# First layer of a four-layer graph kernel: which engine makes the constants, which steps of the plan are urgent, and what the normed tiles wait for

## Chip, cores and metric

The kernel runs on one core of a Trainium2 chip. The metric is the time of one execution on the device, in microseconds (us); lower is better. A profile comes from one further execution, whose span runs from the first to the last instruction that the profiler recorded. The core has five engines with queues of their own: TensorE (PE, with its weight loads as PEld), VectorE (DVE), ScalarE (ACT), GpSimd (POOL) and SyncE (SP, which issues the DMAs).

## What is computed

The input x is 128 graphs of 64 nodes with 256 features, in float32, and an adjacency matrix of 64 by 64. Four layers follow each other, each of the form x + f(relu(layernorm(x))). The change lies in the first one:

```python
h = jnp.maximum(_layernorm(x, axis=-1), 0.0)
A_norm = A + jnp.eye(n)
deg = jnp.sum(A_norm, axis=0) + jnp.sum(A_norm, axis=1) - jnp.diagonal(A_norm)
dinv = jax.lax.rsqrt(deg)
A_hat = A_norm * dinv[:, None] * dinv[None, :]
agg = jnp.einsum('nm,bmd->bnd', A_hat, h)
h1 = relu(batchnorm(agg @ W1.T + b1))        # 512 wide, over all rows
x = x + batchnorm(h1 @ W2.T + b2)
```

The second layer needs all eigenvectors of the normalized Laplacian of the same matrix (`eigh` of a 64 by 64 matrix). The third has four small LSTMs, the fourth an attention over edges; neither is touched by the change.

## The kernel before

**Tiling.** The 8192 rows of x are 16 blocks of 512 rows. A block is four tiles of 128 rows, each with two graphs, and stays in SBUF. A_hat is applied to a tile with a matrix of 128 by 128 that has A_hat twice on its diagonal (BDH). For one block, the first half of layer 1 (`hidden_block`) does this: four normed tiles on ScalarE (`relu`, written into z), eight matmuls with BDH for each half of the features (`mix`), a copy of the result into z on ScalarE, eight matmuls of 512 columns with W1 (`product`), statistics of these on VectorE (bn_stats into st1) and a copy on ScalarE. When all blocks are done, the statistics are put together, and `features0` does the products with W2.

**Layernorm's scales.** `norms` makes the scales (r, m) for a group of blocks: four bn_stats for each block, and then a dependent chain of twelve small steps, one of them a square root on ScalarE. Groups are block 0, blocks 1 to 3, and three of four blocks. In the trace the tiles of this chain are called m_st, m_d, m_v, m_y, m_r and m_m.

**The eigenvectors** are a long serial chain of small steps beside this: `adjacency` makes the Laplacian S out of the degrees, `tridiagonal` turns it around with the matrix JR and does some 61 Householder steps (`householder`), then `vectors` finds values, vectors and a verdict (k_badi). At the end of the stage a branch reads the verdict and would run a slower method if it failed. The second layer starts after the branch.

**What sets the order.** The class `Plan` lays the instructions of TensorE, VectorE and ScalarE out by hand, before any is emitted, with estimated costs: `busy` is how long a step holds its engine, `ready` when its result can be used. `chain` places a step of the eigenvector chain at once. `beside` puts a step into its engine's queue. Before each step of the chain, `fill` places queued steps as long as they fit before the time at which the chain's step is due, with a tolerance (0.6 us on TensorE, 0.3 on the two others). An urgent step is preferred, and needs only to start before that time. `fill` looks at the first 12 entries of a queue. `event(t)` is a need that is met at planned time t. A step's needs count in the plan alone; the real waits come from the tiles that it reads and writes.

**The start.** `constants` makes index vectors with iota on GpSimd, and copies of parts of the identity matrix and some small index arithmetic on VectorE. It is emitted before the plan and isn't part of it. `adjacency` copies the identity matrix twice more (self.I2, called I in the trace). `rs`, `cs` and `dg` are row sums, column sums and the diagonal of the adjacency matrix. `dg`'s step writes the tile `junk` (f_a_junk). The steps of A_hat come last in `adjacency`: An is A + I, dd[:, 1] the diagonal matrix of dinv, `hat` a matmul of the two, Ah its scaled result, `both` a matmul that repeats it on both halves, and two copies write BDH.

The needs of the four normed tiles of a block are the scales, the products of three blocks before (for the buffer z), and `mixes`, which is the second of the BDH copies.

```python
if at is not None and (at + x.busy <= until + self.slack[engine] or x.urgent and at <= until):
    if best is None or (not x.urgent, at) < best[:2]:
        best = not x.urgent, at, x
```

```python
h = [beside("S", lambda j=j: relu(j), needs, 0.52, 0.6) for j in range(TPB)]
mixed = []
for dc in range(2):
    bank = []
    x = beside("T", lambda dc=dc: mix(dc), h, 0.98, 1.1, bank)
```

Of the kernel before, what the change touches and what calls it, by code (L numbers as in the profile page):

```python
# [11 lines left out]
ALU = mybir.AluOpType  # L12
# [900 lines left out]
class Fast:  # L913
# [36 lines left out]

    def constants(self):
        o, nc, k, t = self.o, self.nc, self.k, self.t
        iota = lambda x, pat, base, m: nc.gpsimd.iota(x, pattern=pat, base=base, channel_multiplier=m,
                                                      allow_small_or_imprecise_dtypes=True)
        ident = k.ident
        self.J = t("J", 128, 64)
        iota(self.J[:], [[1, 64]], 0, 0)
        self.P = t("P", 64, 1)  # L960
        iota(self.P[:], [[0, 1]], 0, 1)

        self.TR, self.TC = t("TR", 64, 64), t("TC", 64, 1)
        iota(self.TR[:], [[-1, 64]], 63, 0)
        iota(self.TC[:], [[0, 1]], 63, -1)
        self.JR = t("JR", 64, 64)
        o.copy(self.JR[:], ident[:64, 63::-1])
        self.I2 = t("I2", 64, 128)
        o.copy(self.I2[:, 0:64], ident[:64, :64])
        o.copy(self.I2[:, 64:128], ident[:64, :64])  # L970

        self.q, self.uw, self.ME = t("q", 128, 18, 4, 2), t("uw", 128, 4, 2), t("ME", 128, 2, 64)
        for x, v in ((self.q[:, 0, :, 0], 0.0), (self.q[:, 0, :, 1], 1.0), (self.q[:, 1, :, 0], 1.0),
                     (self.q[:, 1, :, 1], 0.0), (self.uw[:, 0, 0:1], 1.0), (self.uw[:, 0, 1:2], 0.0),
                     (self.ME[:, 1, 0:1], 0.0), (t("DR", 128, 2, 64)[:, 1, 63:64], 0.0)):
            nc.gpsimd.memset(x, v)
        self.I2T = t("I2T", 128, 64)
        o.copy(self.I2T[0:64, :], ident[0:64, 0:64])
        o.copy(self.I2T[64:128, :], ident[64:128, 64:128])
        self.one = t("one", 64, 64)  # L980
        nc.vector.memset(self.one[:], 1.0)
        self.low = t("low", 64, 64)
        o.ts(self.low[:], self.J[:64, :], self.P[:], ALU.is_lt)

        self.par = t("par", 64, 1)
        pi, pj = t("pi", 64, 1, dt=I32), t("pj", 64, 1, dt=I32)
        o.copy(pi[:], self.P[:])
        o.ts(pj[:], pi[:], 1, ALU.bitwise_and)
        o.copy(self.par[:], pj[:])
        o.ts(self.par[:], self.par[:], -2.0, ALU.mult, 1.0, ALU.add)  # L990

        self.dl = 4.0 / (GRID * GRID + 1)
        self.h = self.dl / (GRID - 2)
        X = self.X0 = t("X0", 128, 64)
        iota(X[0:64, :], [[1, 64]], 1, 64)
        iota(X[64:128, :], [[1, 64]], 1, 64)
        o.ts(X[:], X[:], self.dl, ALU.mult, -2.0, ALU.add)
        self.HN = t("HN", 128, 64)
        o.ts(self.HN[:], self.J[:], -0.5, ALU.add, self.h, ALU.mult)

# [463 lines left out]
class Kernel:  # L1466
# [60 lines left out]
    def adjacency(self, fast, plan):  # L1527


        nc, o = self.nc, self.o  # L1530
        t = lambda n, *s: fast.t("a_" + n, N, *s)
        I = self.ident[:N, :N]
        self.I2 = self.c("I2", N, P)
        o.copy(self.I2[:, 0:N], I)
        o.copy(self.I2[:, N:P], I)
        self.S = self.c("S", N, N)
        self.BDH = self.c("BDH", P, P)
        self.BDA, self.BDU, self.BDUT = (self.c(n, P, P) for n in ("BDA", "BDU", "BDUT"))
        nc.vector.memset(self.BDH[:], 0.0)
        for bd in (self.BDA, self.BDU, self.BDUT):  # L1540
            nc.gpsimd.memset(bd[:], 0.0)
        rs, cs, dg, deg, junk = t("rs", 1), t("cs", 1), t("dg", 1), t("deg", 2), t("junk", N)
        di, dm, pos, y, r = t("di", 2), t("dm", 2), t("pos", 1), t("y", 2), t("r", 2)
        dd, An, Ah, L = t("dd", 2, N), t("An", N), t("Ah", N), t("L", N)
        V = lambda emit, *needs, busy=0.09, ready=0.22: plan.chain("V", emit, needs, busy, ready)
        now = {}

        def keep(name, a, b, p=64):
            now[name] = fast.mm((a, b), p=p)

        came = plan.chain("T", lambda: None, (), 0.0, 3.0)
        d = V(lambda: o.red(rs[:], self.A[:], ALU.add), came)
        d = V(lambda: o.red(cs[:], self.AT[:], ALU.add), came)
        g = V(lambda: o.stt(junk[:], self.A[:], 1.0, I, ALU.mult, ALU.mult, acc=dg[:]), came, busy=0.2, ready=0.3)
        d = V(lambda: o.add(cs[:], cs[:], rs[:]), d)

        d = deg0 = V(lambda: o.sub(deg[:, 0:1], cs[:], dg[:]), d, g)
        d = V(lambda: o.ts(deg[:, 1:2], deg[:, 0:1], 1.0, ALU.add), d)
        m = d = V(lambda: o.ts(dm[:], deg[:], 1e-30, ALU.max), d)
        q = plan.chain("S", lambda: self.act(y[:], dm[:], AF.Sqrt), [d], 0.13, 0.25)  # L1560
        l = V(lambda: o.add(L[:], self.A[:], self.AT[:]), came)
        l = V(lambda: o.ts(L[:], L[:], -0.5, ALU.mult), l)
        l = V(lambda: o.stt(L[:], I, deg[:, 0:1], L[:], ALU.mult, ALU.add), l, deg0, ready=0.3)
        z = V(lambda: o.ts(pos[:], deg[:, 0:1], 0.0, ALU.is_gt), deg0)
        d = V(lambda: o.recip(r[:], y[:]), q)
        d = V(lambda: o.mul(r[:], r[:], dm[:]), d)
        d = V(lambda: o.add(r[:], r[:], y[:]), d)
        d = V(lambda: o.recip(r[:], r[:]), d)
        d = h = V(lambda: o.ts(di[:], r[:], 2.0, ALU.mult), d)
        d = z = V(lambda: o.mul(di[:, 0:1], di[:, 0:1], pos[:]), d, z)  # L1570
        d = V(lambda: o.ts(dd[:, 0, :], I, di[:, 0:1], ALU.mult), d, busy=0.15, ready=0.28)
        d = plan.chain("T", lambda: keep("s", L[:], dd[:, 0, :]), [d, l], 0.3, 0.5)
        made = V(lambda: o.ts(self.S[:], now["s"][:], di[:, 0:1], ALU.mult), d, busy=0.15, ready=0.28)

        V = lambda emit, *needs: plan.beside("V", emit, needs, 0.15, 0.3)
        a = V(lambda: o.add(An[:], self.A[:], I), came)
        d = V(lambda: o.ts(dd[:, 1, :], I, di[:, 1:2], ALU.mult), h)

        def hat():
            now["h"] = fast.psv.tile([P, N], F32, name="fvps")  # L1580
            self.mm(now["h"][:N, :], An[:], dd[:, 1, :])

        def both():
            now["b"] = fast.psv.tile([P, N], F32, name="fvps")
            self.mm(now["b"][:], self.I2[:], Ah[:])

        d = plan.beside("T", hat, [a, d], 0.3, 0.5)
        d = V(lambda: o.ts(Ah[:], now["h"][:N, :], di[:, 1:2], ALU.mult), d)
        d = plan.beside("T", both, [d], 0.3, 0.5)
        d = V(lambda: o.copy(self.BDH[0:64, 0:64], now["b"][0:64, :]), d)  # L1590
        return made, V(lambda: o.copy(self.BDH[64:128, 64:128], now["b"][64:128, :]), d)

    def eigenvectors(self):
# [2 lines left out]
        self.U, self.UT = self.c("U", N, N), self.c("UT", N, N)  # L1596
        with ExitStack() as ex:
            fast = Fast(self.tc, ex, self)
            fast.constants()
            plan = Plan(dict(T=0.6, S=0.3, V=0.3), 5)  # L1600
            made, mixes = self.adjacency(fast, plan)
            self.open0(ex)
            self.hidden0(plan, mixes)
# [187 lines left out]
    def hidden0(self, plan, mixes):  # L1791

        pool, used, banks = self.p0, {}, []
        for lo, hi in ((0, 1), (1, 4), (4, 8), (8, 12), (12, 16)):
            r, m, steps = self.norms(pool, range(lo, hi))
            came = [plan.event(4.5 + 1.5 * (i + (i > 0))) for i in range(lo, min(hi, 4))]
            d, first = [], (hi - lo) * TPB
            for n, (engine, emit) in enumerate(steps):
                if n < first:
                    d.append(plan.beside(engine, emit, [came[n // TPB]] if came else [], 0.36, 0.45, urgent=not lo))  # L1800
                else:
                    d = [plan.beside(engine, emit, d, 0.12, 0.25, urgent=not lo)]
            for i in range(lo, hi):
                banks += self.hidden_block(i, r[:, i - lo], m[:, i - lo], plan, d + used.get(i - 3, []) + [mixes], used)
        self.features0(plan, banks, used)

    def hidden_block(self, i, r, m, plan, needs, used):
        nc, pool, psum, W1 = self.nc, self.p0, self.ps0, self.W0[0]
        beside, now = plan.beside, {}

# [17 lines left out]
        mixed = []  # L1828
        for dc in range(2):
            bank = []  # L1830
            x = beside("T", lambda dc=dc: mix(dc), h, 0.98, 1.1, bank)
            x = beside("S", lambda dc=dc: self.act(now["z"][:, 2 + dc, :], now["m", dc][:], AF.Copy), [x], 0.55, 0.65)
            bank.append(x)
            mixed.append(x)
# [952 lines left out]
```

## Time and profile before

| | |
|---|---|
| Time before, median of 3 runs | 2326.83 us (2326.06 to 2328.2) |
| Profiled execution, its own time | 2326.85 us |
| Its span | 2325.1 us |
| First layer and eigenvectors, to the branch | 0 to 370.1 us |
| TensorE busy in 0 to 10 / 10 to 15 / 15 to 20 us | 1.03 / 1.88 / 4.42 us |
| TensorE busy in 100 to 300 us | 195.2 us |
| Loads of x, W1 and W2 | DMA engines full from 10 to 30 us, near 350 GB/s |
| Householder steps | from 11.5 to 272 us |
| Last product with W1 to first product with W2 | 208.3 to 217.6 us |

Line 799 is a helper that records every operation of the three ordered engines, so instructions are told apart by tiles: out<-in, with the names of the program. A row of a timeline has the start, the duration, the engine, the operation, shapes and how many instructions were merged, and in brackets the idle time of its engine before it with what ended it. A float32 matmul of the eigenvector chain shows up as two records, as does a product of 512 columns.

### The profile page before, as it was taken

The page shows a single profiled execution, that of the slowest core. Times are in us where ns is not written, and L with a number is a line of the kernel's source. Part 1 is how long each engine was busy: PE and PEld are TensorE (multiplying, and loading weights), DVE is VectorE, ACT ScalarE, POOL GpSimd, SP SyncE. Part 2 cuts the span into 40 slices and gives each one's busy share as a digit, 9 for nine tenths or more (in the row PEclk, how much of TensorE's full clock was granted, in tenths as well). Part 3 has the DMA queues.
Part 4 walks back from the last instruction along what each step waited for, and adds up shares of the span by engine and source line. Part 5 has one row for each costly group of instructions (what it writes and reads, how often), then busy time and mean ns, then how long its engine had stood idle before and what let it go on. Part 6 is the DMA issues. An engine that isn't in the chain of part 4 may idle for free.

```text
span 2325.1 us, 32725 instructions
## 1 busy us (share of the span) xinstructions
PE 2283.6 (98%) x12169; PEld 1633.1 (70%) x12169; DVE 1629.3 (70%) x4054; ACT 1139.5 (49%) x2483; POOL 3.0 (0%) x26
## 2 busy tenths in 40 slices
PE   7999998999999999999999999999999999999999
PEld 4554445676777788888999998888885544554544
DVE  8887676888447777666767676559756686766667
ACT  5765865754436654433444444336435544444321
POOL 0000000000000000000000000000000000000000
PEclk9999999999999999999999999999999999999999
DMA  5000211230000000001000002000010000000001
GB/s 171 1 1 26 65 56 30 71 83 19 1 37 0 1 19 1 1 1 37 1 1 1 1 1 73 1 1 17 1 46 28 1 5 15 15 19 14 14 24 46
DMA packets 61065, 54.81 MB, mean 24 GB/s; under 512 B 15203, under 2 KB 58724, under 8 KB 60900
## 3 DMA queue, kind: packets, MB, share of 16 engines
q1 hardware_dynamic: 60900, 52.66, 7.4%
q8 instruction: 97, 1.59, 0.3%
q14 instruction: 68, 0.56, 0.1%
HBM read 35.86 MB, written 16.78 MB: 23 GB/s over the span
## 4 chain that ended last, share of the span: by engine, by line
PE 79%; DVE 3%; issue 1%; ACT 1%; DMA 0%; SPq 0%; ACTq 0%; DVEq 0%
PE ps L799 69%; PE acc L799 5%; PE pt L799 4%; PE pe L799 1%; PE y L799 1%; DVE aw L799 1%; DVE X L799 1%; DVE sm_m L799 0%; DVE XV L799 0%; ACT ls_g L799 0%; ACT h L799 0%; DVE ls_g L799 0%; ACT big L799 0%; DVE ls_t L799 0%; DVE sm_e L799 0%
## 5 line engine op out<-in xcount | busy, mean ns | idle before, releaser
L799 ACT ACTIVATE ls_g<-ls_g,ls_b 128x512 f32<-128x512 f32 (+4 forms) x472 | 243.1, 565 | 151.4 <-DVE ls_g L799 149.6
L799 ACT ACTIVATE ls_g<-ps,ls_b 128x256 f32<-128x256 f32 (+3 forms) x268 | 115.5, 470 | 330.9 <-PE ps L799 327.7
L799 PE MATMUL ps<-z,w 128*128 128x512 f32 x512 | 254.9, 621 | 0.9 <-ACT z L799 0.9
L799 PE MATMUL ps<-big,X 128*128 128x176 f32 (+3 forms) x848 | 212.7, 366 | 0.1
L799 DVE TENSOR_TENSOR ls_g<-ls_z,ps 128x512 f32<-128x512 f32 (+5 forms) x256 | 146.8, 579 | 91.9 <-PE ps L799 90.4
L799 DVE TENSOR_TENSOR aw<-at,ed_OST 128x1024 f32<-128x1024 f32 x128 | 149.9, 1219 | 83.0 <-PE ps L799 82.8
L799 PE MATMUL ps<-ls_tx,X 128*128 128x160 f32 (+2 forms) x960 | 206.8, 326 | 0.6 <-ACT ls_g L799 0.6
L799 PE MATMUL ps<-X,X 128*128 128x160 f32 (+1 forms) x896 | 199.1, 306 | 0.0
L799 PE MATMUL ps<-X,ls_w 128*128 128x256 f32 x640 | 190.5, 379 | 0.0
L799 PEld LDWEIGHTS ps<-ls_tx,X 128*128 128x128 f32 x960 | 161.8, 190 | 15.1 <-DVE X L799 4.8
L799 PEld LDWEIGHTS ps<-big,X 128*128 128x128 f32 x848 | 145.9, 190 | 29.7 <-issue 19.4
L799 DVE TENSOR_TENSOR X<-ls_g 128x1024 f32<-128x1024 f32 (+2 forms) x108 | 117.4, 1087 | 49.9 <-ACT ls_g L799 49.8
L799 ACT ACTIVATE r<-ps 128x512 f32<-128x512 f32 x256 | 131.6, 614 | 41.5 <-PE ps L799 41.4
L799 PEld LDWEIGHTS ps<-X,X 128*128 128x128 f32 x896 | 148.4, 190 | 0.0
L799 PE MATMUL ps<-X,ls_s 128*128 128x256 f32 x480 | 142.3, 379 | 0.0
L799 PEld LDWEIGHTS ps<-z,w 128*128 128x128 f32 x512 | 87.2, 190 | 69.0 <-issue 60.2
L799 PE MATMUL ps<-ls_tx,ls_s 128*128 128x256 f32 x464 | 134.8, 379 | 0.0
L799 PE MATMUL ps<-ed_S,Q 64*128 64x512 f32 x512 | 132.9, 618 | 1.4 <-DVE hT L799 0.7
L799 PE MATMUL ps<-ls_tx,ls_w 128*128 128x256 f32 x464 | 133.2, 380 | 0.0
L799 PEld LDWEIGHTS ps<-X,ls_w 128*128 128x128 f32 x640 | 121.4, 190 | 16.8 <-DVE X L799 0.3
L799 PE MATMUL ps<-big,ls_w 128*128 128x256 f32 x464 | 131.9, 379 | 0.7 <-ACT ls_z L799 0.7
L799 PE MATMUL ps<-aw,ed_ODT 128*64 128x512 f32 x512 | 117.3, 595 | 0.1
(545 smaller groups left out, 4019.0 us busy)
## 6 DMA issues: line engine op xcount, KB each, us to landing
X<-in_x_dram SPq DMA_DIRECT2D x32, 512.0 KB
xs<-X SPq DMA_DIRECT2D x16, 512.0 KB
X<-xs SPq DMA_DIRECT2D x16, 512.0 KB
out_dram<-X SPq DMA_DIRECT2D x31, 256.0 KB
X<-in_L_gnn_Wih_t_dram SPq DMA_DIRECT2D x4, 512.0 KB
ls_w<-in_L_gnn_Wih_t_dram SPq DMA_DIRECT2D x4, 512.0 KB
ls_w<-in_L_gnn_Whh_t_dram SPq DMA_DIRECT2D x4, 512.0 KB
w<-in_L_gnn_W_t_dram SPq DMA_DIRECT2D x2, 512.0 KB
```

Of the source, the lines that this page charges most:

```text
L799: i = method(*a, **kw)
```

## The change

Seven copies of the identity matrix move from VectorE to ScalarE. Seven other small constants become steps beside the chain that may not start before planned time 25, or after the one that they read. The five VectorE steps and two TensorE steps of A_hat are made urgent. The normed tiles of a block no longer have `mixes` among their needs; the matmuls that read BDH have it instead. The plan is made before the constants, so that they can be queued in it.

```diff
-    def constants(self):
+    def constants(self, plan):
...
-        o.copy(self.JR[:], ident[:64, 63::-1])
+        self.act(self.JR[:], ident[:64, 63::-1], AF.Copy)
         self.I2 = t("I2", 64, 128)
-        o.copy(self.I2[:, 0:64], ident[:64, :64])
-        o.copy(self.I2[:, 64:128], ident[:64, :64])
+        self.act(self.I2[:, 0:64], ident[:64, :64], AF.Copy)
+        self.act(self.I2[:, 64:128], ident[:64, :64], AF.Copy)
...
-        o.copy(self.I2T[0:64, :], ident[0:64, 0:64])
-        o.copy(self.I2T[64:128, :], ident[64:128, 64:128])
+        self.act(self.I2T[0:64, :], ident[0:64, 0:64], AF.Copy)
+        self.act(self.I2T[64:128, :], ident[64:128, 64:128], AF.Copy)
...
-        o.ts(self.low[:], self.J[:64, :], self.P[:], ALU.is_lt)
+        spare = lambda emit, *needs: plan.beside("V", emit, needs or [plan.event(25.0)])
+        spare(lambda: o.ts(self.low[:], self.J[:64, :], self.P[:], ALU.is_lt))
...
-        o.copy(pi[:], self.P[:])
-        o.ts(pj[:], pi[:], 1, ALU.bitwise_and)
-        o.copy(self.par[:], pj[:])
-        o.ts(self.par[:], self.par[:], -2.0, ALU.mult, 1.0, ALU.add)
+        d = spare(lambda: o.copy(pi[:], self.P[:]))
+        d = spare(lambda: o.ts(pj[:], pi[:], 1, ALU.bitwise_and), d)
+        d = spare(lambda: o.copy(self.par[:], pj[:]), d)
+        spare(lambda: o.ts(self.par[:], self.par[:], -2.0, ALU.mult, 1.0, ALU.add), d)
...
-        o.ts(X[:], X[:], self.dl, ALU.mult, -2.0, ALU.add)
+        spare(lambda: o.ts(X[:], X[:], self.dl, ALU.mult, -2.0, ALU.add))
...
-        o.ts(self.HN[:], self.J[:], -0.5, ALU.add, self.h, ALU.mult)
+        spare(lambda: o.ts(self.HN[:], self.J[:], -0.5, ALU.add, self.h, ALU.mult))
...
-        o.copy(self.I2[:, 0:N], I)
-        o.copy(self.I2[:, N:P], I)
+        self.act_copy(self.I2[:, 0:N], I)
+        self.act_copy(self.I2[:, N:P], I)
...
-        V = lambda emit, *needs: plan.beside("V", emit, needs, 0.15, 0.3)
+        V = lambda emit, *needs: plan.beside("V", emit, needs, 0.15, 0.3, urgent=True)
...
-        d = plan.beside("T", hat, [a, d], 0.3, 0.5)
+        d = plan.beside("T", hat, [a, d], 0.3, 0.5, urgent=True)
         d = V(lambda: o.ts(Ah[:], now["h"][:N, :], di[:, 1:2], ALU.mult), d)
-        d = plan.beside("T", both, [d], 0.3, 0.5)
+        d = plan.beside("T", both, [d], 0.3, 0.5, urgent=True)
...
-            fast.constants()
             plan = Plan(dict(T=0.6, S=0.3, V=0.3), 5)
+            fast.constants(plan)
...
-                banks += self.hidden_block(i, r[:, i - lo], m[:, i - lo], plan, d + used.get(i - 3, []) + [mixes], used)
+                banks += self.hidden_block(i, r[:, i - lo], m[:, i - lo], plan, d + used.get(i - 3, []), [mixes], used)
...
-    def hidden_block(self, i, r, m, plan, needs, used):
+    def hidden_block(self, i, r, m, plan, needs, mixes, used):
...
-            x = beside("T", lambda dc=dc: mix(dc), h, 0.98, 1.1, bank)
+            x = beside("T", lambda dc=dc: mix(dc), h + mixes, 0.98, 1.1, bank)
```

## Prediction

> **What bounds the kernel now.** I read the page's table of busy time first, then its 40 slices, then the opening (timeline, busy time by stretches), then the end of the first layer, where a branch closes the stage that the change touches.
>
> ```profile
> PE 2283.6 (98%) x12169; PEld 1633.1 (70%) x12169; DVE 1629.3 (70%) x4054; ACT 1139.5 (49%) x2483; POOL 3.0 (0%) x26
> PE   7999998999999999999999999999999999999999
> ...
> 0.00:10.00 10.00, 1.03 (x5) 0.66 (x6) 6.47 (x48) 1.49 (x2) 2.21 (x23) 1.00 0.67 221
> 10.00:15.00 5.00, 1.88 (x12) 1.38 (x13) 4.05 (x29) 1.19 (x7) 0.00 (x0) 1.00 1.10 350
> 15.00:20.00 5.00, 4.42 (x21) 4.00 (x22) 4.58 (x23) 3.54 (x11) 0.00 (x0) 1.00 1.10 348
> 20.00:25.00 5.00, 4.70 (x21) 3.04 (x20) 4.40 (x28) 2.13 (x9) 0.00 (x0) 1.00 1.10 348
> 25.00:30.00 5.00, 5.00 (x18) 2.14 (x17) 3.79 (x18) 3.92 (x12) 0.00 (x0) 1.00 1.10 349
> ```
>
> Stretch rows give PE, PEld, DVE, ACT, POOL busy, then clock, DMA share, GB/s. TensorE is full everywhere but in the first slice. From about 20 us on the layer is bound by TensorE; before that TensorE waits for its first real work. What that work waits for is in the timeline (start, duration, then idle time before it):
>
> ```profile
> 3.62 0.21 DVE L799 TENSOR_REDUCE f_a_cs<-AT 64x1 f32<-64x64 f32 x1 [0.53 <-DMA AT<-in_adj_t_dram]
> 3.76 0.18 DVE L799 TENSOR_SCALAR f_HN<-f_J 128x64 f32<-128x64 f32 x1
> 3.86 0.18 DVE L799 COPY f_JR<-ident 64x64 f32<-64x64 f32 x1
> 4.17 0.39 DVE L799 COPY f_I2T<-ident 64x64 f32<-64x64 f32 x2
> 5.16 0.21 DVE L799 SCALAR_TENSOR_TENSOR f_a_junk<-A,ident 64x64 f32<-64x64 f32 x1
> 6.11 0.20 ACT L799 ACTIVATE f_a_y<-f_a_dm 64x2 f32<-64x2 f32 x1 [4.09 <-DVE f_a_dm L799]
> 8.66 0.28 DVE L799 TENSOR_SCALAR S<-fps,f_a_di 64x64 f32<-64x64 f32 x1 [0.56 <-PE fps L799]
> 14.64 0.15 DVE L799 SCALAR_TENSOR_TENSOR m_m<-m_m,m_r 128x4 f32<-128x4 f32 x1
> 15.73 0.26 ACT L799 ACTIVATE f_ja<-f_x 64x62 f32<-64x62 f32 x1 [1.92 <-DVE f_x L799]
> 16.69 2.06 ACT L799 ACTIVATE z<-X,m_m,m_r 128x256 f32<-128x256 f32 x4
> 16.79 0.23 DVE L799 COPY BDH<-fvps 64x64 f32<-64x64 f32 x1
> 17.33 3.98 PE L799 MATMUL ps<-BDH,z 128*128 128x128 f32 x16 [0.58 <-ACT z L799]
> 21.34 0.60 ACT L799 ACTIVATE z<-ps 128x512 f32<-128x512 f32 x1 [1.11 <-PE ps L799]
> 22.52 4.56 PE L799 MATMUL ps<-z,w 128*128 128x512 f32 x10
> ```
>
> The reader is to see three things. Between the column sums (3.62) and the diagonal's sum (5.16), both on VectorE, stand constants that the diagonal doesn't need. The block's scales are ready at 14.79 (m_m), and ScalarE then sits idle for 1.92 us, yet the four normed tiles start at 16.69, when the last copy of A_hat's matrix (BDH) is due. And the matmuls of block 0 follow the normed tiles directly.
>
> The end of the stage:
>
> ```profile
> 360.72 3.70 PE L799 MATMUL ps<-z,w 128*128 128x512 f32 x8
> 364.66 0.15 DVE L799 CAST f_k_badi<-fps 64x1 int32<-64x1 f32 x1 [0.98 <-PE fps L799]
> 366.41 0.17 DVE L799 TENSOR_SCALAR bn_b<-bn_b 128x2 f32<-128x2 f32 x1
> 370.13 3.32 PEld L799 LDWEIGHTS ps<-ones,ident 128*128 128x128 f32 x16 [5.59 <-issue]
> ```
>
> The layer's products end at 364.42, the eigenvectors' verdict is written at 364.81, VectorE's tail ends at 366.58, and the branch takes the rest to 370.13. So two chains end within half a microsecond of each other, and both must come earlier for the branch to come earlier. In the same stage (20 to 365 us) the waits of TensorE's matmuls that the trace names add up to 9.7 us (3.7 of it for the eigenvalue chain's f_v), so the plan has some play of its own.
>
> **What the Trainium skill says.** "ScalarE: Activation LUTs", section "Table sets: the hidden batching unit", says that cheap functions such as copy are in every table set. The trace agrees as far as it goes: one table load (0.74 to 2.02), then Sqrt, Square, Copy and Relu until 365 without another. The same page, "What ACT_TABLE_LOAD costs", gives 1283 ns and about 1380 ns of drain for a switch of sets; the trace has 1.28 us for the load. "TensorE: Matmul & The Clock Gate", section "What's actually happening", says that a cold array runs at half rate until about 3.4 us of sustained work. The trace agrees: block 0's sixteen 128x128 matmuls take 3.98 us, later groups of eight take 1.16 us.
>
> **The change part by part.**
>
> *Constants off VectorE.* Seven copies go to ScalarE; seven tensor-scalar and cast steps (HN, low, pi, X, pj and two on par) become late steps of the plan. The diagonal's sum needs A, ident and its place behind the column sums, so it can start where HN did: 5.16 - 3.76 = 1.40 us earlier. The next steps are a dependent chain up to S (8.66), so all of it moves by 1.40, and S is written from 7.26. The arrival of AT at 3.62 is next in line and does not move. On ScalarE the seven copies run from 2.02: small copies there start about 0.10 us apart (12.10, 12.21, 12.30, 12.40), so they are done near 2.9, against a square root due at 6.11 - 1.40 = 4.71. They are hidden by ScalarE's 4.09 us of idle time. If the first Copy drew another table set, a second load would end at 2.9 + 1.28 = 4.2 (hidden), or at 5.6 with the drain that the skill gives (0.9 us lost). I take none and keep 0.9 for the range.
>
> *The late constants.* Their durations are 0.18, 0.25, 0.14, 0.18, 0.14, 0.14 and 0.14: 1.17 us of VectorE after planned time 25. VectorE idles 1.21 us in 25 to 30 and 0.63 us in 30 to 35, so I cost them at nothing; without that cover they delay the eigenvalue chain by at most 1.2 us. Until then they hold 7 of the 12 places that the planner looks at. The other five are enough: the entries behind them are statistics and a dependent chain, taken one after the other. By hand I find none held back that is due.
>
> *A_hat urgent.* An, dd, Ah and the two BDH copies (0.20, 0.24, 0.27, 0.22, 0.23 us, about half of that when pipelined) and two matmul pairs move from 9.5 to 17.0 into the first 3 us after S. They go partly ahead of block 0's statistics, which costs these 0.3 to 0.5 us. Laying out the order by hand from the planner's costs, I find the last step of the scales, m_m, in its old place, between f_v and f_x of the first Householder step, since the gaps of that step absorb the delay. Both BDH copies then end long before the normed tiles. Ah (14.72) and BDH (16.17, 16.79) no longer stand between the chain's steps: about 0.3 to 0.4 us less there.
>
> *Normed tiles free of the matrix.* They need m_m alone. One of four (0.49 us apart: 2.06 us for four with the last one's end) fits into the 1.92 us before the square at 15.73; the planner lets only 0.3 us run over, so the other three stay behind the next f_z. That is 0.5 us. The mixing matmuls follow the fourth tile, and the z copy and the first product follow them.
>
> *Sum.* 1.40 + 0.35 + 0.5 = 2.25 us, say 2.3: mixes end at 19.0 instead of 21.3, the first product starts at 20.2 instead of 22.5. The half-rate phase moves along, since it starts with the same burst. Block 0's eight products (16 records) keep TensorE fed to about 28.5; block 1 needs the scales of blocks 1 to 3, whose statistics follow block 0's and come about 2 us earlier too. X arrives at 350 GB/s, 1.5 us for a block of 0.52 MB; block 0's statistics would start at 7.5, when (from the 2.2 MB moved by 10 us) X0 is there. No queue of SP or POOL is moved past.
>
> After that TensorE is full, so the rest of the layer shifts as a whole, products by 2.3 us. The eigenvalue chain gets at least the 1.40; by hand one product now slips ahead of the third Householder step's matmuls, so it keeps 1.5 to 2.1. The end of the stage moves by something between. I take 2.4, allowing a little for the play in those 9.7 us of waits: 2326.83 - 2.4 = 2324.4. The profiled execution took 2326.85 (span 2325.1), so working against it or the median comes to the same.
>
> **The rivals.** *Given back (0.13).* The products gain 2.3 us but the verdict gains only what the chain keeps, and loses about a microsecond to products placed ahead of its matmuls: 0 to -1.2, about 2326.2. For it: verdict and products end 0.4 us apart. Against: the last verdict steps wait for VectorE, not TensorE.
>
> *Better laid plan (0.28).* The shift lets waits inside the stage fall away: a third of the 9.7 us besides the 2.3 gives -5.5, 2321.3. For it: single waits of 1.3 to 1.5 us, for f_v, f_PB and f_w_g, depend on where a product falls. Against: nothing directs them.
>
> *Worse laid plan (0.11), the slower side.* Each of some 61 Householder steps has two matmul pairs before which the planner may place products that run 0.6 us over. With products ready earlier, 0.12 us more per step makes the chain 7.3 us later; less the 1.4 of the opening, and with products absorbing some, +5: 2331.8. It decides once the verdict falls behind VectorE's tail, that is if the chain loses more than 366.58 - 364.81 = 1.8 us against the products. For it: products stand ahead of f_v's matmuls at 27.01 and 30.70. Against: TensorE's total work is unchanged.
>
> **How the numbers follow.** The forecast has 0.48, its own range is -1.0 to -4.0 (the 0.9 of a table load and 0.5 of a tile off, 1.5 of play on): 2322.8 to 2325.8. About 0.2% (4.65 us) is what a measurement of this kernel can tell from no change. Forecast and "given back" fall inside it, 0.61; the better plan is faster, 0.28; the worse is slower, 0.11. The range 2320.3 to 2327.6 leaves out the worse plan and the far end of the better one.
>
> **What would show it.** S written near 7.3; JR, I2 and I2T on ScalarE before 3.5 with one table load; the last BDH copy before 11; the first normed tile near 13.3; the first product near 20.2; products ending near 362 and the branch done near 367.8. A first product later than 21.5 refutes the sum of the opening. If it starts at 20.2 and the branch still ends at 370, the shift was lost within the stage. A second table load before 5 us would take up to 0.9. The prediction is wrong if the plan's later order decides more than the opening does.

## The result, and the profile after

| | before | changed |
|---|---|---|
| Median of the runs, 20 of each | 2328.57 us (2323.59 to 2333.9) | 2323.86 us (2322.33 to 2327.48) |
| Profiled execution, its own time | 2326.85 us | 2323.89 us |
| Its span | 2325.1 us | 2322.0 us |

The ratio of the two is 0.998, with a 95% interval of 0.9974 to 0.9986: 4.7 us less, between 3.3 and 6.05. The 20 runs of the kernel before, among them the three known ahead of the prediction, have a higher median than those three (2326.83), and spread over 10 us, those of the changed kernel over 5. In a later comparison, with seven runs of the changed kernel against 41, the ratio was 0.9975 (0.9964 to 0.9986). So the change gains about 0.2%; about half of the 4.7 us was predicted.

The opening in the changed kernel's timeline (start, duration, then in brackets idle time of the engine before it and what ended it). The 16 records of the mixes are eight matmuls with BDH, four for each half of the features:

```profile
3.32 0.21 DVE L799 TENSOR_REDUCE f_a_cs<-AT 64x1 f32<-64x64 f32 x1 [0.28 <-DMA AT<-in_adj_t_dram]
3.42 1.28 ACT L799 ACT_TABLE_LOAD   x1
3.46 0.21 DVE L799 SCALAR_TENSOR_TENSOR f_a_junk<-A,ident 64x64 f32<-64x64 f32 x1
4.71 0.20 ACT L799 ACTIVATE f_a_y<-f_a_dm 64x2 f32<-64x2 f32 x1
4.89 0.14 DVE L799 TENSOR_SCALAR f_a_pos<-f_a_deg 64x1 f32<-64x1 f32 x1
4.95 0.15 DVE L799 RECIPROCAL f_a_r<-f_a_y 64x2 f32<-64x2 f32 x1
6.90 0.28 DVE L799 TENSOR_SCALAR S<-fps,f_a_di 64x64 f32<-64x64 f32 x1 [0.56 <-PE fps L799]
9.70 0.23 DVE L799 COPY BDH<-fvps 64x64 f32<-64x64 f32 x1
13.31 0.15 DVE L799 SCALAR_TENSOR_TENSOR m_m<-m_m,m_r 128x4 f32<-128x4 f32 x1
13.49 1.09 ACT L799 ACTIVATE z<-X,m_m,m_r 128x256 f32<-128x256 f32 x2 [1.01 <-DVE m_m L799]
15.10 3.78 PE L799 MATMUL ps<-BDH,z 128*128 128x128 f32 x16
15.16 1.08 ACT L799 ACTIVATE z<-X,m_m,m_r 128x256 f32<-128x256 f32 x2
19.42 2.08 PE L799 MATMUL ps<-z,w 128*128 128x512 f32 x2
```

The diagonal's sum (f_a_junk) starts 0.14 us behind the column sums instead of 1.54, S comes at 6.90 instead of 8.66 (0.30 of it because AT arrived earlier), and the mixes start at 15.10 instead of 17.33. The first product starts at 19.42 instead of 22.52, but its two records take 2.08 us; a pair at full rate takes 1.13. The end of the stage:

```profile
358.52 3.70 PE L799 MATMUL ps<-z,w 128*128 128x512 f32 x8
362.46 0.15 DVE L799 CAST f_k_badi<-fps 64x1 int32<-64x1 f32 x1 [0.98 <-PE fps L799]
364.22 0.17 DVE L799 TENSOR_SCALAR bn_b<-bn_b 128x2 f32<-128x2 f32 x1
368.03 3.49 PEld L799 LDWEIGHTS ps<-ones,ident 128*128 128x128 f32 x16 [5.69 <-issue]
```

Products, verdict and VectorE's tail all come 2.2 us earlier, the branch 2.1 us. Behind it 0.8 us are given back by 1742 us, and more than that is won again at the start of layer four, where the weight loads of one step take 3.06 us before and 1.59 after. First the kernel before, then the changed one:

```profile
1747.72 3.06 PEld L799 LDWEIGHTS ps<-w_t,hS 128*128 128x128 f32 x8 [1.79 <-DVE hS L799]
```

```profile
1746.46 1.59 PEld L799 LDWEIGHTS ps<-w_t,hS 128*128 128x128 f32 x8 [2.04 <-DVE hS L799]
```

The code there is the same in both. A stretch in which TensorE's instructions take about twice as long is called a half-rate phase here. The granted clock shows this one: 0.77 in 1740 to 1750 us and 0.89 in 1750 to 1760 before, 1.00 after.

### The profile page after: what moved, and what is told of

Read it like the earlier page. It is cut to its first block, busy times and chain, and to the rows that moved or that the text cites. A ratio compares the mean times of both kernels' runs of the same rounds, so it can differ in the third digit from the quotient of the medians.

```text
span 2322.0 us, 32728 instructions
## 1 busy us (share of the span) xinstructions
PE 2282.6 (98%) x12169; PEld 1631.9 (70%) x12169; DVE 1629.0 (70%) x4047; ACT 1141.8 (49%) x2491; POOL 2.9 (0%) x26
## 3 DMA queue, kind: packets, MB, share of 16 engines
q8 instruction: 97, 1.59, 0.3%
## 4 chain that ended last, share of the span: by engine, by line
PE 79%; DVE 3%; ACT 1%; issue 1%; DMA 0%; ACTq 0%; DVEq 0%
PE ps L799 69%; PE acc L799 5%; PE pt L799 4%; PE pe L799 1%; PE y L799 1%; DVE aw L799 1%; DVE X L799 1%; DVE sm_m L799 0%; DVE XV L799 0%; ACT ls_g L799 0%; ACT h L799 0%; DVE ls_g L799 0%; DMA X<-in_L_gnn_Wih_t_dram 0%; DVE ls_t L799 0%; DVE big L799 0%
```

## The experiments

Two theories stood at the start. Theory A: the opening gives its 2.1 us in every run, and the rest of the 4.7 is where half-rate phases of TensorE happen to fall, layer four's start above all. Rival B: the first layer of the kernel before is slower in most runs than in the one profiled. The first four kernels ran together, with 67 runs of the kernel before (median 2328.37, 2323.29 to 2334.15).

**The kernel before once more, unchanged, for a second profile.**

> The kernel before, once more. Theory A (the opening gives about 2.1 us, and the rest of the measured 4.7 us lies in where the array's half-rate phases fall, at the start of layer four above all): ratio 1.000 within 0.001, runs spread over several us, the branch closes at 370.1 within 0.4 in its trace, and the stretch from 1743 to 1760 us is either slow (weight loads of 0.33 us, as in the trace of before) or fast, which moves the span by about 1.7. Rival B (the first layer of before is itself slower in most runs than in the one profiled): the branch closes later than 371.

Measured: 2329.09 us, ratio 1.000 (0.9992 to 1.0009). The profiled execution has a span of 2330.4, and its branch was done at 375.07 us, 4.9 later than in the first profile. So Theory A's 370.1 is missed, and what B says is there: the first layer varies. Layer four starts at full rate in this profile, so it isn't what makes it long. Both profiles have the same instructions with nearly the same waits; here is one place in the second profile, TensorE's timeline, and then the same place in the first:

```profile
117.65 0.24 PE L799 MATMUL fps<-f_v,f_uk 1*41 1x41 f32 x2 [1.16 <-DVE f_v L799]
...
117.90 1.88 PE L799 MATMUL ps<-z,w 128*128 128x512 f32 x2
```

```profile
115.89 0.24 PE L799 MATMUL fps<-f_v,f_uk 1*41 1x41 f32 x2 [1.16 <-DVE f_v L799]
...
116.13 1.13 PE L799 MATMUL ps<-z,w 128*128 128x512 f32 x2
```

After the same wait of 1.16 us the next product takes 1.88 us in one run and 1.13 in the other. The busy time by stretches, with the granted clock in the column before the last two, tells where such phases lie. In the second profile of before:

```profile
110.00:120.00 10.00, 8.85 (x48) 4.74 (x48) 7.77 (x37) 7.67 (x27) 0.00 (x0) 0.91 0.01 2
120.00:130.00 10.00, 10.00 (x43) 4.99 (x42) 6.32 (x30) 6.12 (x21) 0.00 (x0) 0.92 0.00 1
...
220.00:230.00 10.00, 10.00 (x30) 3.98 (x29) 4.55 (x25) 5.86 (x20) 0.00 (x0) 0.66 0.37 107
```

In the first profile of before:

```profile
190.00:200.00 10.00, 8.59 (x41) 4.37 (x41) 6.80 (x36) 4.90 (x19) 0.00 (x0) 0.96 0.01 2
200.00:210.00 10.00, 10.00 (x43) 4.62 (x42) 6.52 (x31) 4.46 (x16) 0.00 (x0) 0.87 0.00 0
```

One minus the clock, times 10 us, is the time lost in a stretch that TensorE fills: 0.9 + 0.8 = 1.7 and then 3.4 us in the second profile, 0.4 + 1.3 = 1.7 in the first. Where TensorE also waits, less is lost: at layer four's start the clock's 3.4 us are 1.8 us in the instructions. In every profile of this study the losses come in such steps of 1.7 us (up to the last 20 us of the span), as 3.4 us at half rate would give. Behind the branch, from 360 to 380 us, the first profile of before loses one step and that of the changed kernel two, which is in line with the 0.8 us given back there. The Trainium skill, "TensorE: Matmul & The Clock Gate", section "What's actually happening", has a free-running window of about 3.4 us by which the clock is set; the traces agree with the length, and with the page's remark that the place varies from run to run. That section has the clock drop after at least one idle window of that length; here the drops come behind much shorter waits, in a stage that is otherwise full.

Of all profiles of this study, ten are of kernels without fills (those with fills come further down). They have twelve half-rate phases between 30 and 360 us, two of them twice as long as the others. In each of them the first slow product starts within 1.8 us of the end of a wait of 0.85 to 1.41 us. But the length of a wait alone doesn't decide. Waits of 1.45 and 1.3 us stand near the end of every layout, and in no profile does a half-rate phase lie between them and the branch. In the second profile of before, the later of the two and its stretch:

```profile
353.33 0.40 PE L799 MATMUL fps<-f_DR,ident 64*64 64x128 f32 x2 [1.28 <-DVE f_w_g L799]
```

```profile
350.00:360.00 10.00, 8.72 (x22) 3.71 (x21) 8.61 (x56) 2.68 (x9) 0.00 (x0) 1.00 0.03 11
```

**Constants alone.** Only the constants' part of the change:

```diff
-        o.copy(self.JR[:], ident[:64, 63::-1])
+        self.act(self.JR[:], ident[:64, 63::-1], AF.Copy)
...
+        spare = lambda emit, *needs: plan.beside("V", emit, needs or [plan.event(25.0)])
```

> The constants alone (seven copies on ScalarE, seven steps late), A_hat and normed tiles as before. Theory A: S is written near 7.1, 1.4 us earlier against the column sums; the normed tiles still wait for BDH and start about 1.4 earlier, near 15.2; the branch closes 0.8 to 1.5 earlier than before, near 369; a second table load as in the changed kernel. If the constants carry all of the gain: 2.1 earlier.

Measured: 2325.37 us, ratio 0.9988 (0.9981 to 0.9994). S at 6.92, first normed tile at 14.94, mixes at 15.58 (the second half of them only at 19.17). The branch was done at 369.5, 0.6 us earlier than in the first profile of before, a little less than expected. About half of the gain or more is in this part.

**The two other parts without it** (A_hat urgent, normed tiles freed):

```diff
-        V = lambda emit, *needs: plan.beside("V", emit, needs, 0.15, 0.3)
+        V = lambda emit, *needs: plan.beside("V", emit, needs, 0.15, 0.3, urgent=True)
...
-            x = beside("T", lambda dc=dc: mix(dc), h, 0.98, 1.1, bank)
+            x = beside("T", lambda dc=dc: mix(dc), h + mixes, 0.98, 1.1, bank)
```

> A_hat urgent and the normed tiles free, constants on VectorE as before. Theory A: S stays at 8.7, the normed tiles start near 14.9, the first mixing matmuls near 16.5, the branch closes 0.6 to 1.0 us earlier than before, near 369.3. If the constants carry all: no gain, 370.1.

Measured: 2330.33 us, ratio 1.001 (1.0004 to 1.0016), slightly slower than before, which neither expectation had. In its profile a block of products stands behind the verdict's matmul, so that the statistics and the branch come late. Which of the two parts does it was asked next.

**The changed kernel with one table load.** A square root of a single number ahead of the copies, so that the first load already has the square root's set:

```diff
+        root = t("root", 1, 1)
+        self.act(root[:], k.ones[0:1, 0:1], AF.Sqrt)
         self.JR = t("JR", 64, 64)
```

> The changed kernel with one Square-root step of a single number first on ScalarE, so that only one set of tables is loaded. Theory A: the square root of the degrees starts 0.4 us earlier (right after its input) but VectorE was busy until 0.04 us before the result is used, so S moves by 0.05 us at most and the time stays: ratio to before as the changed kernel, 0.998. If the second load costs its full 1.28 us: 1.3 us faster than the changed kernel, branch near 366.8 instead of 368.0.

Measured: 2323.77 us, ratio 0.9976 (0.997 to 0.9983); the changed kernel had 2323.86 in its own comparison. This profile has one load. S at 6.92, as with two loads. The second load of the changed kernel (3.42 to 4.70) delays the square root, which could start at 4.30, by 0.4 us, but VectorE is busy with L and f_a_pos until it reads the root at 4.95, so nothing waits. The load is hidden.

The next four ran together, with 40 runs of the kernel before (median 2327.31). **A_hat urgent alone, and normed tiles freed alone**, the two halves of the diff of A_hat and the tiles above:

> A_hat's steps urgent, all else as in the kernel before. Theory (a late block of products): the two edits together left three products behind the layer's verdict and took 2330.3; one of the edits alone is enough for it. If it is this one, the last block of products before the verdict is shorter than the eight records of before, a block of some six follows the verdict, the branch is done 4 to 5 us after the verdict's read (before: 5.5 to 5.7 us after it, with nothing left), and the median lies 2 to 3 us above the kernel before's. Rival (half-rate phases of TensorE made the difference): the block before the verdict has eight records as before and the median lies within 1 us of the kernel before's.

> Normed tiles freed of A_hat's matrix, all else as in the kernel before. Theory (a late block of products): as for the run with A_hat's steps urgent; if this edit is the one that leaves three products behind the verdict, 2330 to 2331 and a block of products behind the verdict; if neither does alone, both lie within 1 us of the kernel before's and the two edits have to come together. Rival (half-rate phases made the difference): no products behind the verdict in either, medians within 1 us of the kernel before's. With the tiles freed the first normed tile should be near 14.3 us and the first product near 21.5 to 22.

Measured: A_hat urgent alone 2329.73 us, ratio 1.0008 (1.0 to 1.0016); normed tiles freed alone 2326.1 us, ratio 0.9993 (0.9983 to 1.0002). The profile of A_hat alone, TensorE and VectorE at the end of the stage:

```profile
366.66 0.27 PE L799 MATMUL fps<-f_k_bad,ones 64*64 64x1 f32 x2
...
366.87 2.84 PE L799 MATMUL ps<-z,w 128*128 128x512 f32 x6
...
371.38 0.19 DVE L799 TENSOR_REDUCE bn_a<-sums 128x2 f32<-128x32 f32 x1 [4.26 <-DVEq L1618]
...
374.00 0.19 DVE L799 TENSOR_REDUCE bn_b<-sums 128x2 f32<-128x32 f32 x1 [1.76 <-ACT ps L799]
```

Three products (six records) come behind the verdict. The branch lets VectorE go at 371.38, after 4.26 us of idle time, as expected, but the last statistics still have to follow: their reduction starts at 374.00. So layer two's first matmuls start 7.35 us behind the verdict's, where the kernels without this block have 5.76 to 5.91. Freeing the tiles alone has eight records before the verdict and none behind it. So A_hat's urgency makes the late block, and the constants' part undoes it in the whole change. That the block costs time is plain in the profile; how much isn't, as the median's interval begins at no loss. The freed tiles' first one came at 14.69 and the first product at 20.94, 0.4 later and 0.6 earlier than expected.

**Filling TensorE's waits.** If half-rate phases follow waits, matmuls on constants in the plan's gaps should prevent them. In the kernel before, and in the changed one, `chain` places these before a step of TensorE, from the third Householder step on in the kernel before and from the first in the changed one:

```diff
+        if engine == "T" and self.heat is not None:
+            at = self.start(x)
+            while at - self.free["T"] > 0.25:
+                self.place(Step("T", self.heat, (), 0.25, 0.25, None), self.free["T"])
...
+            for _ in range(2):
+                nc.tensor.matmul(now["w"][:], self.k.ident[:], self.k.ones[:, 0:64], start=True, stop=True)
```

> The kernel before, with matmuls on constants put into the gaps that the plan leaves on TensorE ahead of its chain steps (ten pairs or so more in the whole first layer; results are not read). Theory (half-rate phases follow TensorE's waits of 0.7 to 1.5 us in the first layer, and make most of the spread of the kernel before): no half-rate stretch near 116 to 120 us or 200 to 230 us, the median falls from about 2328.5 to 2324 to 2326 and the spread from 10 us to 6. Rival (the half-rate phases fall where they fall, whatever TensorE waits for): half-rate stretches as before, median within 1 us of the kernel before's, or up to 2 us above it for the added matmuls.

> The changed kernel with the same matmuls in the plan's gaps (some fifteen pairs, those of the opening among them). Theory (half-rate phases follow waits): TensorE at full rate by 18 us instead of 24.4, so that the products gain up to 2.2 us, no half-rate stretch in the first layer, median 2321 to 2323 against 2323.9 for the changed kernel. Rival (phases fall where they fall): median 2323.5 to 2325.

Measured: 2336.39 us (1.0038, 1.0024 to 1.0051) and 2344.79 us (1.0072, 1.0052 to 1.0091). Both medians are misses, and the reason is the fill itself. In the filled kernel before the group of added matmuls is

```profile
L800 PE MATMUL fvps<-ones,ident 128*128 128x64 f32 x112 | 14.1, 275 | 0.0
```

112 records, four for each pair, are 28 fills of 0.50 us, where the plan reckoned 0.25: 7 us too much. The verdict stands 338.9 us behind the matmuls of the fourth Householder step (its reflector has 60 entries, 1*60 in the trace) instead of 333.6 and 336.7 in the two profiles of before. In the changed kernel's opening it is worse: 60 records take 13.06 us at half rate from 10.84 on, planned at 3.75. From then on TensorE doesn't wait, and yet it is still at half rate more than 20 us later:

```profile
10.84 13.06 PE L800 MATMUL fvps<-ones,ident 128*128 128x64 f32 x60
...
34.40 0.41 PE L800 MATMUL fps<-f_A 61*64 61x61 f32 x2
...
38.99 0.32 PE L800 MATMUL fps<-f_v,f_uk 1*61 1x61 f32 x2
```

The pair at 34.40 takes 0.28 us at full rate, and the one at 38.99 is at full rate. So a TensorE that the trace shows as busy doesn't always leave half rate within 3.4 us, as the section of the Trainium skill that the prediction cites has it: this run doesn't agree with it.

But the other half of the theory held in the kernel before. The stretch of the filled kernel before where the second profile of before had its phase:

```profile
110.00:120.00 10.00, 10.00 (x58) 6.21 (x57) 7.86 (x36) 8.87 (x28) 0.00 (x0) 1.00 0.00 1
120.00:130.00 10.00, 10.00 (x44) 4.61 (x43) 6.49 (x33) 5.90 (x23) 0.00 (x0) 1.00 0.00 1
```

The clock stays at 1.00 in all stretches from 30 to 360 us. The filled changed kernel has one half-rate phase there, with 1.7 us lost in 40 to 50 us, among its added matmuls and without a wait ahead of it; so a wait isn't the only thing that a phase can follow.

**The fill at its price**, with the last four kernels and 41 runs of the kernel before (median 2327.12): one matmul instead of two, only in gaps over 0.4 us, from the fourth Householder step on.

> The kernel before, with one matmul on constants (two records of some 117 ns, planned at 0.25 us) in each planned gap over 0.4 us of TensorE ahead of its chain steps in the first layer, from the fourth Householder step on. The run with pairs showed that no half-rate window came between 30 and 360 us once TensorE never waited, but its pairs took 0.47 us each where the plan had 0.25, so that it lost 9 us. Theory (waits bring half-rate windows, which cost the kernel before about 2 us in the median): with the dummies at their planned price the waits at 94.7, 115.9 and 197.4 us are filled at no loss, no half-rate window follows them, and the median falls 1 to 4 us below the kernel before's. Rival (the gaps are needed by work of other engines, and filling them delays the chain by as much as it saves): median within 1 us of the kernel before's, although the windows are gone.

> The changed kernel with the same single matmuls in its planned gaps over 0.4 us, from the fourth Householder step on. Theory (waits bring half-rate windows): the changed kernel has fewer such waits left (those at 115, 195 and 215 us), so the gain is smaller than for the kernel before: median 0 to 2 us below the changed kernel's 2323.9. Rival (filling costs what it saves): 2323.5 to 2325.

Measured: before with fills 2327.89 us (0.9996, 0.9987 to 1.0004), changed with fills 2324.43 us (0.9987, 0.998 to 0.9993). In the medians the rival is right, filling gains nothing. In the spread the theory is right for the kernel before: its 13 runs with fills end at 2328.89, while 12 of the 41 runs of before are above 2329, up to 2333.14. The lowest rises by 1.0 us, from 2323.32 to 2324.29. Half-rate phases are gone from 30 to 360 us in both profiles, and the fill costs 0.6 to 0.9 us in each (the table below).

**The changed kernel once more, and the change without A_hat's part:**

> The changed kernel once more, for a second profile. Theory A (opening 2.1 to 2.4 us earlier, the rest of the 4.7 us is fewer half-rate windows in the layer, since the waits at 94.7 and 115.9 us are gone from its layout): median within 1 us of 2323.9, no half-rate window between 90 and 140 us, branch done at 366 us plus what half-rate windows this run shows. Rival B (the one profile of it happened to be a good one): a half-rate window between 90 and 140 us here as in the kernel before's second profile, branch done after 370 us.

> The change without its middle part: constants moved and normed tiles freed, A_hat's steps not urgent. The parts alone gave: constants 0.9988, tiles freed 0.9993, A_hat urgent 1.0008. Theory (the parts add, and A_hat's urgency costs through the layout): 0.9981 minus what A_hat's loss is, thus about 0.9975 to 0.9982, no worse than the whole change's 0.998. Rival (A_hat's urgency is of use once the constants are off VectorE, since the copies into BDH come at 9.7 us instead of near 15 and let the mixes start): 0.9985 to 0.999, mixes starting 0.4 to 1 us later than the change's 15.1 us.

Measured: changed again 2322.91 us (0.9975, 0.9964 to 0.9986), without A_hat's urgency 2323.79 us (0.9978, 0.9969 to 0.9987). Rival B, here that the changed kernel's one profile was a good one by chance, isn't borne out: its second profile has no half-rate stretch from 30 to 360 us either, and its branch was done at 365.28. A_hat's urgency shows no worth in the whole: without it the mixes start at 15.08 us, as with it, although the last BDH copy comes at 14.71 instead of 9.70. The scales (m_m) are then 0.42 us earlier, at 12.89, since the statistics have VectorE to themselves.

The second profile of the changed kernel shows one more thing, TensorE in the opening:

```profile
18.96 1.13 PE L799 MATMUL ps<-z,w 128*128 128x512 f32 x2
...
20.38 3.70 PE L799 MATMUL ps<-z,w 128*128 128x512 f32 x8
...
28.23 0.28 PE L799 MATMUL fps<-f_v,f_uk 1*60 1x60 f32 x2 [0.45 <-DVE f_v L799]
```

In the first profile of it:

```profile
22.04 4.70 PE L799 MATMUL ps<-z,w 128*128 128x512 f32 x8
...
30.88 0.28 PE L799 MATMUL fps<-f_v,f_uk 1*60 1x60 f32 x2 [0.45 <-DVE f_v L799]
```

The same pair of records took 1.13 us here and 2.08 there, eight took 3.70 and 4.70, and the matmuls of the reflector of 60 entries come 2.65 us apart. How long the opening stays at half rate changes from run to run, and the whole layer shifts with it.

**All profiles in one table.** Start of the mixes; start of the matmuls of the reflector of 60 entries, in the fourth Householder step (by then every profile is at full rate); time lost by the granted clock from 30 to 360 us; start of the verdict's matmul; and the verdict less the reflector and the loss, which is what the layout itself takes.

| kernel | mixes | reflector 60 | lost | verdict | layout |
|---|---|---|---|---|---|
| before, first | 17.33 | 30.71 | 1.7 | 364.35 | 331.9 |
| before, second | 17.17 | 32.47 | 5.1 | 369.16 | 331.6 |
| before with fills | 17.01 | 32.43 | 0 | 364.97 | 332.5 |
| A_hat urgent alone | 17.16 | 32.57 | 3.4 | 366.66 | 330.7 |
| A_hat urgent and tiles freed | 17.23 | 32.44 | 5.1 | 368.08 | 330.5 |
| tiles freed alone | 17.04 | 30.34 | 3.4 | 364.84 | 331.1 |
| constants alone | 15.58 | 30.82 | 1.7 | 363.70 | 331.2 |
| changed, first | 15.10 | 30.88 | 0 | 362.15 | 331.3 |
| changed, second | 15.19 | 28.23 | 0 | 359.49 | 331.3 |
| changed, one table load | 15.11 | 28.20 | 3.4 | 362.72 | 331.1 |
| changed with fills | 15.21 | 28.56 | 0 | 360.73 | 332.2 |
| changed without A_hat | 15.08 | 31.03 | 0 | 362.29 | 331.3 |

The last column is the same to 0.3 us in the two profiles of one kernel, although the verdicts of before differ by 5. So a verdict is the sum of three things: when the opening is through, which has an early and a late value, 1.8 us apart in the two profiles of before and 2.7 in those of the changed kernel; half-rate phases of 1.7 us each; and a layout that the change shortens by 0.3 to 0.6 us. (The two kernels with pairs of fills are left out.)

## Why the prediction was right or wrong

**The time** was predicted as 2324.4 us and came to 2323.86, in the range. That the two agree to 0.5 us is in part luck: the forecast was 2.4 us less than three runs of before, and the gain came to 4.7 us (3.3 to 6.05) against 20 runs. Taken as a gain, it is beyond the forecast's own 1.0 to 4.0 us. The steps:

**Constants off VectorE, 1.40 us: right.** From the column sums to S it was 5.04 us, and is 3.58: 1.46 less. The constants alone give S the same place. The seven copies took until 3.40, not the 2.9 reckoned, and that too is hidden.

**No second table load: wrong, at no cost.** With the copies first there are two loads of 1.28 us, at 0.73 and 3.42; with a square root first there is one. The Trainium skill, "ScalarE: Activation LUTs", section "What ACT_TABLE_LOAD costs", adds about 1380 ns of drain, which would have cost 0.9 us; this trace shows the load between the last copy and the root at once, with no such gap. The hidden case among those worked out is what happened.

**Late constants at nothing:** not shown; no run takes them apart from the copies. Constants alone are faster than before, which bounds a loss but doesn't show that there is none.

**A_hat urgent, 0.35 us: wrong.** It shows nothing in the whole change, and a loss by itself (ratio 1.0008, about 2 us, with an interval from 1.0), by another way than the chain's loss in the rival of a worse laid plan: the chain there is shorter (330.7), and products are left over behind the verdict. The prediction had them as steps that only move out of the way; in the plan they also push the statistics of block 0, by 0.42 us at m_m, about the 0.35 that they were to save.

**Normed tiles, one of four ahead of the square, 0.5 us: right in kind, too small by one tile.** Two fit (13.49), two stay behind f_z (15.16), and from m_m to the mixes it is 0.90 us less than before. The 1.92 us of idle time were read wrongly on the way: they run from 13.82 to 15.73, and only 0.94 of them lie behind the scales (14.79). In the changed kernel two tiles fill the same place, from 13.49 to the square at 14.49.

**The sum, 2.3 us to the mixes and the first product: right for the start.** The mixes start 2.23 us earlier in the first profiles, 1.93 without AT's earlier arrival: 1.46 for the constants and 0.90 for the tiles, less 0.43 by which the scales follow S later. So the A_hat term was too high and the tiles term too low, and the agreement with 2.25 owes as much to AT. The first product started 3.1 us earlier than in the first profile of before, as one product slipped ahead of the third Householder step's matmuls.

**"The half-rate phase moves along, since it starts with the same burst": this step failed.** The burst did move by 2.2 us, the phase didn't go with it. Weight loads take 0.28 us or more at half rate, where 0.19 is full rate; the first ones of 0.19 come at 22.15 us in the first profile of before, and at 24.42 in that of the changed kernel. At reflector 60 the changed kernel was 0.17 us later than before (30.88 against 30.71). The pair of first profiles sets an early opening of before against a late one of the changed kernel, and has none of the gain: its 2.2 us at the verdict are 1.7 us of a half-rate phase at 190 to 210 us that the changed kernel didn't have and 0.6 of layout. That the branch came 2.1 us earlier where 2.4 was predicted is an agreement of sums, not of terms. Taken over the table, with like openings compared, the mechanism does hold: late against late it's 32.43 to 32.57 without the constants' part and 30.82 to 31.03 with it, 1.4 to 1.75 us less; early against early 30.34 (tiles freed) and 30.71 (before) against 28.20 to 28.23 (28.56 with a fill ahead of it), 2.1 to 2.5 us less. The lowest runs say the same: 2320.68 for the changed kernel and 2323.32 for before in one comparison, 2.6 us.

**"After that TensorE is full, so the layer shifts as a whole": right in the order, wrong in what full means.** Waits of 9.7 us in a stage of 345 were counted as play. They are also the places behind which half-rate phases begin. In the layout of before it waits 0.65 us at 94.66 and 1.16 us at 115.89; in the changed one the first is gone and the second is

```profile
115.34 0.24 PE L799 MATMUL fps<-f_v,f_uk 1*41 1x41 f32 x2 [0.73 <-ACT z L799]
```

Of the four profiles with a wait of 1.15 us or more near 115 to 120 us (before twice, A_hat alone, the two parts without constants), three have a half-rate phase between 110 and 130; none of the six with 0.73 us has (constants alone, tiles freed alone, the changed kernel twice, with one table load, without A_hat). The runs fit: above 2329 us lie 9 of the first 20 runs of before and 54 of the 148 beside the experiments, but none of 27 of the changed kernel, none of 11 without A_hat, 1 of 21 with constants alone and 2 of 14 with the tiles freed alone. The mean granted clock, which is on record for every run, puts a number on it. It is given to three places, too coarse for one run, but an average over many says something: one minus the clock, times the span, is 7.8 us over the 148 runs of before and 5.9 over the 27 of the changed kernel. So of the 4.7 us between their mean spans, about 1.9 are time lost by the clock, somewhere in the kernel, and 2.8 are the rest, opening and layout. With fills in the kernel before, the lost time falls from 7.4 us (the 41 runs beside it) to 5.9, and the rest grows by 0.9, the price of the fill; in the changed kernel with fills it doesn't fall (5.3 with fills and without). That phases follow waits is thus supported from two sides. That these two waits, at 94.66 and 115.89, are what made the difference isn't proved, as no run takes them alone.

**The rivals.** "Better laid plan" came true in its direction and not its size: the named waits fell by 0.8 us, from 9.7 to 8.9, not by a third, and their worth lies in the half-rate phases more than in themselves. "Given back" is not seen: verdict and products move together. "Worse laid plan" happened to one part alone.

**Open.** Waits of 1.41 us near 196 and 0.85 near 215 are in the changed layout too, and after them the profile with one table load lost 3.4 us while both profiles of the changed kernel lost nothing; what decides there wasn't found. Nor was it found why of the five profiles with constants moved and tiles freed one has a half-rate phase at layer four's start (with fills), and of the seven others four (those with pairs of fills left out): the code there is the same.

**A better version** than the changed kernel did not come out. One table load and A_hat's old priorities are each within its interval.

## What to carry to other kernels

Where a stage is full on TensorE, what comes before it counts in full, so shorten the chain to the first large burst, and check by undoing each part that all parts of a change pull: here the constants did most, and one part gained nothing in the whole and cost time by itself. Waits of about a microsecond inside a full stage can cost more than their length, because half-rate phases can follow them; look at the granted clock in stretches of 10 us. Matmuls made to fill such gaps brought nothing here; whether useful work in them would was not tried. Before a difference of a few microseconds between two profiles is explained, profile both kernels twice and set the terms beside each other; one pair gave the right sum here with the wrong parts.

## What the hardware showed that was not expected

The granted clock stands at 1.00 in the opening of every profile, although a pair of records takes 2.08 us there and 1.13 later, so the first half-rate phase must be read from durations. In the changed kernel that phase was over by 18.6 us in one profile and at 24.4 in the other, and the work behind it stood 2.65 us apart. In one run with fills, 13 us of matmuls on constants did not end it. And the loss by the granted clock comes in multiples of 1.7 us: 3.4 over the span up to its last 20 us in both profiles of the changed kernel, 6.8 and 10.2 in those of before.
